# Attention pipeline of a macaron block: where the reciprocal, the cosine product and the side work stand

## The chip, the cores and the metric

The kernel runs on one core of a Trainium2 chip. The metric is the device time of one execution in microseconds (us), the median of several runs. All arithmetic is in 32-bit floating point.

Engines by their names in the profile: PE is TensorE (matrix products and transposes; PEld its weight loads), DVE is VectorE, ACT is ScalarE, POOL is GpSimd, SP is SyncE, which only issues transfers here. Each engine works through its own queue of instructions in the order in which the program wrote them.

## The reference

The input is x, 4 sequences of 512 tokens with 256 features. Three sublayers follow one another, each on a layer-normalised x:

```
x = x + 0.5 * ffn(layernorm(x))
x = x + attn(layernorm(x))
x = x + 0.5 * ffn(layernorm(x))
```

The feed-forward part is a mixture of 8 experts of width 512; each token goes to its best two:

```
logits = x @ gate;  w, idx = top_k(logits, 2);  w = softmax(w)
out = sum over e of combine[e] * (silu(x @ w0[e]) * (x @ w1[e])) @ wo[e]
```

The attention has 16 heads with low-rank queries, keys and values and a rotary part:

```
q   = rms_norm(h @ wq_a, q_w) @ wq_b          # per head 64 plain + 64 rotary
ckv = h @ wkv_a                               # 64 low-rank + 64 rotary keys, shared by the heads
kv  = rms_norm(ckv[..., :64], kv_w) @ wkv_b
attn = softmax(query . key * 128**-0.5);  out = (attn @ value) @ wo
```

## The kernel before

**Three stages.** A first feed-forward stage (up to some 300 us of the span), the attention (300 to 905 us), a second feed-forward stage. While attention runs, the routing of the second feed-forward stage is already worked out for batches whose attention is complete (a batch is one sequence of 512 tokens), and the next batch's keys and low-rank queries are prepared. This side work is cut into small parts that are strewn between the steps of attention.

**The attention loop** (L1543 to L1591) walks 64 items, a batch and a head each (`items`), and in each of them 4 places `kc`. Two heads make a pair; the place in the pair is `at`, 0 to 7, and a pair is the unit of the pipeline. In each place the loop writes, in this order:

- a block of scores (`put_scores`): 128 queries against 512 keys on PE, the negative maximum on DVE (L1352), the exponential on ACT (L1354), which also sums its row into `sm`. The block belongs to a head one to one and a half ahead (k = (i+1)*4 + 3 + kc). Place 1 has none, and place 0 has two.
- in place 0 of a pair, the weighing of the values of the two heads before (`put_weigh`, L1380, 16 matrix instructions of PE), its copy (L1444), and the division of the second head of this pair.
- four transposes of a head's probabilities on PE (L1367) and their copy from the accumulator memory, on DVE in even places (L1372), on ACT in odd places (L1374). There are two buffers for the transposes, so those of a place need the copy of two places earlier.
- a few parts of two lists of side work, `asked` and `beside`.

`put_divide(k)` does something only for the last of a head's four blocks, that is in places 0 and 4. It takes the reciprocal of `sm` on DVE (L1359), and four multiplications on POOL (L1361) make the exponentials into probabilities. The head that is divided in place 4 is the first of the next pair; its transposes begin in the next pair's place 0.

There are three buffers for the score blocks and the weighing together (`ps_a`), three for all side work in the accumulator memory (`ps_p`).

**Queries** (`asked`, six parts, added in place 1 for two pairs ahead): the products `pe` and `pn` on PE (L1319); then the cosine product on DVE (L1225) and a copy on ACT (L1326); then a lane shuffle on DVE (L1228) and the other copy; then, on POOL, the sine product (L1230) and two additions (L1232, L1234).

**In pairs with h % 4 == 1** (all even pairs but the very first) the output projection of four heads is written too, half in place 4 and half in place 6 (L1394, 8 matrix instructions each), and its addition on DVE (L1404) one place later.

**The list `beside`** (class `Beside`, L342 to L388) holds generators. `step(n)` runs up to n parts; each part says by what it yields when the next may run:

- a float is the price of the next part: it runs only in a place whose room (`ROOM[at]`) still has that much. Without a float the price is LITTLE, 0.2.
- an int n, or PE_NEXT, or PE_LATE: not before n places (one place for the two names) later.
- `PARTS[at]` is the largest number of parts of a place.

In the feed-forward stages the room is unlimited and `pe_places` names the places at which parts of PE may run; in the attention loop `pe_places` is empty.

From each batch's third head on `beside` is given, in this order: the routing of the batch before (`route_one`: layer norm with `normed`, gate, `choose`), the preparation of the next batch (`prepare`), the indirect writes of the routing (`scatter_one`: 8 small transfers of POOL, L515, each behind a small memset, only in places that are `quiet`), and in the last batch the list of tiles (`listing`, whose first instruction is the copy L888 and whose next is the PE instruction L894). Batch 0 has only the preparation of batch 1.

**Powers.** `inv_sqrt` (L403) takes a power -0.5 on POOL and yields 1; what reads it is the next part: `less` (L408) in `normed`, the product `low` (L1283) in `prepare`.

Of the kernel before, what the change touches and what calls it, by code (L numbers as in the profile page):

```python
# [42 lines left out]
def kernel(  # L43
# [21 lines left out]
    NT = S // P  # L65
# [270 lines left out]

    PE_NEXT, PE_LATE = "pe", "pe late"
    LITTLE = 0.2  # L340

    class Beside:  # L342
# [19 lines left out]
        def step(self, n=1):  # L362

            for _ in range(n):
                if not self.todo or self.count < self.until:
                    return
                if self.pe and self.pe_places:
                    n_ok = 1 if self.pe is PE_LATE else len(self.pe_places)
                    if self.place not in self.pe_places[:n_ok]:
                        return  # L370
                if self.cost > self.room:
                    return
                self.room -= self.cost
                said = next(self.todo[0], self)
                self.pe = said if said in (PE_NEXT, PE_LATE) else False
                self.cost = said if isinstance(said, float) else LITTLE
                if said is self:
                    self.todo.pop(0)
                elif self.pe or isinstance(said, int):
                    self.until = self.count + (1 if self.pe else said)  # L380

        def finish(self):
            self.quiet = True
# [55 lines left out]
    def normed(b, s, store=None, then=None, joint=False):  # L439


        mv = small.tile([P, NT, 2], F32, tag="mv", name="mv")
        if beside.room < math.inf:
            yield 1.2
        for t in range(NT):
            stats(mv, xs[b], t)
            if t % 2:
                yield 1.2 if t == 1 else LITTLE
        var = small.tile([P, NT], F32, tag="var", name="var")
        nc.vector.tensor_scalar_add(var, mv[:, :, 1], LN_EPS)  # L450
        rstd = small.tile([P, NT], F32, tag="rstd", name="rstd")
        yield from inv_sqrt(rstd, var, NT)
        less = minus_mean(mv, rstd)
        yield 0.8
        xn = [xp.tile([P, H2, D], F32, tag="xn", name="xn") for _ in range(2)]
        for half in range(2):
            norm_rows(xn[half], b, half, mv, rstd, less if half else None)
            if half == 0:

                yield 0.6  # L460
        if then is not None:
            then()
        if store is not None:
            for half in range(2):
                store_rows(nc.sync if store else nc.gpsimd, store, b, half, xn[half])
        s["xnT"] = tp.tile([P, DC, S], F32, tag="xnT", name="xnT")

        def turned(half):
            pt = ps_p.tile([P, DC, H2 * P], F32, tag="p", name="pt_ln")
            turn_rows(pt, xn[half])  # L470
            return pt

        def copied(half, pt):
            to = s["xnT"][:, :, half * H2 * P : (half + 1) * H2 * P]
            if half == 0:
                nc.scalar.copy(to, pt)
            else:
                nc.vector.tensor_copy(to, pt)

        yield PE_NEXT  # L480
        first = turned(0)
        if not joint:
            yield
            copied(0, first)
            yield
        second = turned(1)
        yield 0.7
        if joint:
            copied(0, first)
        copied(1, second)  # L490
        yield PE_NEXT
# [746 lines left out]
    def prepare(b):  # L1238

        s = st.setdefault(b, {})  # L1240
        if b == 0:
            nc.vector.tensor_scalar_mul(nwq, nwq, scale)
        yield from normed(b, s)

        pk = ps_p.tile([P, S], F32, tag="p", name="pk")
        for c in range(DC):
            nc.tensor.matmul(
                pk,
                lhsT=wkpe[:, c].rearrange("p u r -> p (u r)"),
                rhs=s["xnT"][:, c, :],  # L1250
                start=(c == 0),
                stop=(c == DC - 1),
            )
        s["k"] = [bp.tile([P, S], F32, tag=f"k{j}", name=f"k{j}") for j in range(2)]
        yield 0.7
        yield from rope(s["k"][1][:ROPE], s["k"][0][ROPE:], pk, xp, "xn")
        yield

        pj = ps_p.tile([P, NT, 2, RANK], F32, tag="p", name="pj")
        for t in range(NT):  # L1260
            for c in range(DC):
                nc.tensor.matmul(
                    pj[:, t].rearrange("p j r -> p (j r)"),
                    lhsT=s["xnT"][:, c, t * P : (t + 1) * P],
                    rhs=wqc[:, c, :],
                    start=(c == 0),
                    stop=(c == DC - 1),
                )
        yield
        sq = xp.tile([P, NT, 2, RANK], F32, tag="xn", name="sq")  # L1270
        nc.scalar.activation(sq, pj, AF.Square)
        yield 0.8
        rr = small.tile([P, NT * 2], F32, tag="rr", name="rr")
        nc.vector.tensor_reduce(
            rr, sq.rearrange("p t j r -> p (t j) r"), AX.X, ALU.add
        )
        ms = small.tile([P, NT * 2], F32, tag="ms", name="ms")
        nc.vector.tensor_scalar(ms, rr, 1.0 / RANK, RMS_EPS, ALU.mult, ALU.add)
        yield
        yield from inv_sqrt(rr, ms, NT * 2)  # L1280
        yield 0.7
        low = bp.tile([P, NT, 3, RANK], F32, tag="low", name="low")
        nc.vector.tensor_tensor(  # L1283
            low[:, :, :2, :],
            pj,
            rr.rearrange("p (t j) -> p t j", j=2).unsqueeze(3).to_broadcast([P, NT, 2, RANK]),
            ALU.mult,
        )
        yield
        nc.gpsimd.tensor_copy(low[:, :, 2, :], low[:, :, 0, :])  # L1290
        s["low"] = low

        s["q"] = bp.tile([P, S], F32, tag="lq", name="lq")
        for i in range(2):
            yield PE_NEXT
            pt = ps_p.tile([P, S], F32, tag="p", name="plow")
            for t in range(NT):
                nc.tensor.transpose(
                    pt[:, t * P : (t + 1) * P],
                    low[:, t, i : i + 2, :].rearrange("p j r -> p (j r)"),  # L1300
                    ident,
                )
            yield 0.7
            a, c = slice(0, RANK), slice(RANK, P)
            hq, hk = (a, c) if i == 0 else (c, a)
            nc.vector.tensor_scalar_mul(s["q"][hq], pt[hq], nwq[hq])
            yield 0.7
            nc.vector.tensor_scalar_mul(s["k"][1 - i][hk], pt[hk], nwk[hk])
        s["ready"] = True
# [103 lines left out]
    def put_queries(p):  # L1413

        if p < n_items // 2:
            b, h = items[2 * p]
            qs[p] = []
            yield from queries(b, h // 2, qs[p])
# [10 lines left out]
    def put_divide(k):  # L1429
        i, t = divmod(k, NT)  # L1430
        if i < n_items and t == NT - 1:
            divide(probs[i], sums.pop(i))
# [104 lines left out]


    PARTS = (5, 2, 1, 1, 1, 1, 1, 2)
    ROOM = (3.2, 1.2, 0.2, 0.2, 0.8, 1.2, 0.8, 1.2)  # L1540
    beside.pe_places = ()
    late = []
    for i, (b, h) in enumerate(items):  # L1543
# [13 lines left out]
        for kc in range(NT):  # L1557

            at = NT * (h % 2) + kc
            beside.at(at, at in (7, 0, 1, 2), LITTLE if late and ROOM[at] < 1.0 else ROOM[at])  # L1560
            k = (i + 1) * NT + LEAD + kc
            if at != 1 or i == 0:
                put_scores(k)
            if at == 0 and i > 0:

                put_scores(k + 1)
                put_weigh(i - 1, range(NT))
                put_divide(k)
                beside.step(PARTS[at])
            pts[i, kc] = turn_probs(probs[i], kc)  # L1570
            for f in late:
                f()
            late.clear()
            if at == 1:
                asked.add(put_queries(i // 2 + 2))
            elif at == 4 and h % 4 == 1 and i > 1:
                late.append(put_out(i - 2, 0))
            elif at == 6 and h % 4 == 1 and i > 1:
                late.append(put_out(i - 2, 1))
                late.append(lambda i=i: finish_x(i - 2))  # L1580
            if kc % 2 == 0:

                asked.step(2 if at == 4 else 1)
            if at != 0 or i == 0:
                put_divide(k)
            if kc % 2:
                asked.step()
            if at != 0:
                beside.step(PARTS[at])
        probs.pop(i)  # L1590
    beside.finish()  # L1591
# [86 lines left out]
```

## Time and profile before

| | us |
|---|---|
| median of 3 runs | 1150.05 (1148.97 to 1151.47) |
| the profiled execution | 1148.07 |
| its span, first to last instruction | 1146.3 |
| PE busy in the span | 1067.8 (93%) |
| POOL, DVE, ACT busy | 586.0, 557.9, 471.9 |
| mean granted clock of PE | 0.980 |

The starts of the query products L1319, one set per pair, give the length of each pair from its place 1 to the next pair's (us, the profiled execution):

| pair of the batch | 0 | 1 | 2 | 3 | 4 | 5 | 6 | 7 |
|---|---|---|---|---|---|---|---|---|
| batch 0 | 16.53 | 18.68 | 21.51 | 17.68 | 18.82 | 16.53 | 18.82 | 16.53 |
| batch 1 | 18.81 | 17.51 | 21.47 | 18.47 | 22.79 | 18.36 | 20.67 | 16.52 |
| batch 2 | 18.82 | 17.50 | 21.18 | 18.48 | 22.79 | 18.37 | 23.30 | 16.53 |
| batch 3 | 18.82 | 17.51 | 21.17 | 17.66 | 29.61 | | | |

A row of the profile's timeline reads: start and duration in us, engine, line and operation, result<-operands, shapes, and in brackets the idle time of the engine ahead of it with what ended that idle time. In a group of instructions the last figures are busy time, mean ns of one, idle time ahead and its releasers. A row of the table by stretches has, behind the stretch's length, the busy time of PE, PEld, DVE, ACT and POOL, the granted clock, the transfers' share and GB/s. PE's instructions overlap in their pipeline, so the duration of one is longer than the distance to the next.

### The profile page before, as it was taken

The page shows a single profiled execution, that of the slowest core. Times are in us where ns is not written, and L with a number is a line of the kernel's source. Part 1 is how long each engine was busy: PE and PEld are TensorE (multiplying, and loading weights), DVE is VectorE, ACT ScalarE, POOL GpSimd, SP SyncE. Part 2 cuts the span into 40 slices and gives each one's busy share as a digit, 9 for nine tenths or more (in the row PEclk, how much of TensorE's full clock was granted, in tenths as well). Part 3 has the DMA queues.
Part 4 walks back from the last instruction along what each step waited for, and adds up shares of the span by engine and source line. Part 5 has one row for each costly group of instructions (what it writes and reads, how often), then busy time and mean ns, then how long its engine had stood idle before and what let it go on. Part 6 is the DMA issues. An engine that isn't in the chain of part 4 may idle for free. (4 is left out here: it accounts for less than half of the span.)

```text
span 1146.3 us, 14713 instructions
## 1 busy us (share of the span) xinstructions
PE 1067.8 (93%) x4738; PEld 600.4 (52%) x4738; DVE 557.9 (49%) x1329; ACT 471.9 (41%) x1030; POOL 586.0 (51%) x655
## 2 busy tenths in 40 slices
PE   4898999999999999999999999999879999999995
PEld 3565555665445554455445545454444556655563
DVE  6453222234557465685656766456735343322221
ACT  4531431222555465645555555455535322144221
POOL 4344455456565455545664447754654236545542
PEclk8998999999999999999999999999989999999998
DMA  9963233322100000100000100001000224323432
GB/s 316 388 139 35 42 49 58 58 38 38 33 1 1 1 1 1 56 1 1 1 2 19 38 1 1 1 1 37 2 5 1 69 51 46 52 37 55 118 51 26
DMA packets 44043, 53.57 MB, mean 47 GB/s; under 512 B 10720, under 2 KB 36704, under 8 KB 43872
## 3 DMA queue, kind: packets, MB, share of 16 engines
q0 software_dynamic: 16960, 22.07, 12.4%
q1 hardware_dynamic: 26736, 30.55, 8.3%
q8 instruction: 40, 0.66, 0.2%
q14 instruction: 35, 0.29, 0.1%
q10 hardware_dynamic: 272, 0.01, 0.0%
HBM read 34.74 MB, written 22.07 MB: 50 GB/s over the span
## 5 line engine op out<-in xcount | busy, mean ns | idle before, releaser
L1344 PE MATMUL ps<-k,q 128*128 128x512 f32 x512 | 262.6, 605 | 5.8 <-POOL q L1232 5.0
L1093 PE MATMUL h<-w_sb,xT 128*128 (+1 forms) x576 | 263.5, 600 | 3.6 <-DVE xT L1061 3.1
L1352 DVE TENSOR_REDUCE nm<-ps 128x1 f32<-128x512 f32 x256 | 173.8, 685 | 92.7 <-PE ps L1344 88.6
L1354 ACT ACTIVATE pr<-ps,nm 128x512 f32<-128x512 f32 x210 | 144.2, 688 | 175.4 <-DVE nm L1352 158.6
L1361 POOL TENSOR_SCALAR pr<-pr,sm 128x512 f32<-128x512 f32 x210 | 142.4, 693 | 71.2 <-DVE sm L1359 51.9
L1367 PEld LDWEIGHTS pt<-ident,pr 128*128 128x128 f32 x840 | 102.1, 142 | 118.7 <-issue 65.3
L1093 PEld LDWEIGHTS h<-w_sb,xT 128*128 128x128 f32 (+1 forms) x576 | 101.4, 186 | 112.8 <-issue 103.4
L1142 POOL DMA_INDIRECT acc_d<-yo,idx x53 | 83.9, 1584 | 148.2 <-DVE yo L1165 74.7
L1129 DVE TENSOR_TENSOR it<-g,h 128x512 f32<-128x512 f32 x72 | 49.5, 688 | 223.7 <-PE h L1093 183.2
L1367 PE MATMUL pt<-ident,pr 128*128 128x128 f32 x840 | 137.7, 277 | 10.8 <-ACT pT L1374 10.2
L1137 ACT COPY iT<-pt_i 128x512 f32<-128x512 f32 x72 | 42.1, 585 | 241.5 <-PE pt_i L1135 241.5
L1093 PE MATMUL py<-w_sb,iT 128*128 (+1 forms) x576 | 136.9, 381 | 2.6 <-ACT iT L1137 1.4
L1230 POOL TENSOR_TENSOR tsin<-tsin,sin_sb 128x512 f32<-128x512 f32 x36 | 46.7, 1296 | 147.9 <-DVE tsin L1228 137.6
L1380 PE MATMUL po<-pT,low 128*64 128x512 f32 x512 | 118.0, 603 | 0.0
L1372 DVE COPY pT<-pt 128x512 f32<-128x512 f32 x128 | 87.3, 682 | 63.0 <-PE pt L1367 62.9
L1093 PEld LDWEIGHTS py<-w_sb,iT 128*128 128x128 f32 (+1 forms) x576 | 100.5, 184 | 19.6 <-ACT iT L1137 2.4
L1344 PEld LDWEIGHTS ps<-k,q 128*128 128x128 f32 x512 | 82.9, 192 | 43.6 <-ACT pT L1374 15.9
L1046 POOL DMA_INDIRECT xg<-xn_d,idx x72 | 72.2, 1003 | 32.4 <-issue 14.1
L1374 ACT COPY pT<-pt 128x512 f32<-128x512 f32 x128 | 74.3, 580 | 18.2 <-PE pt L1367 18.2
L1380 PEld LDWEIGHTS po<-pT,low 128*64 128x64 f32 x512 | 34.2, 138 | 79.9 <-issue 60.1
L1126 ACT ACTIVATE g<-h 128x512 f32<-128x512 f32 x72 | 43.0, 597 | 71.0 <-PE h L1093 67.9
L1165 DVE TENSOR_SCALAR yo<-py,wt 128x256 f32<-128x256 f32 x72 | 34.8, 483 | 65.5 <-PE py L1093 57.3
(234 smaller groups left out, 1328.3 us busy)
## 6 DMA issues: line engine op xcount, KB each, us to landing
w_sb<-in_L_ffn_w_kernel_dram SPq DMA_DIRECT2D x8, 1024.0 KB, 14.2
w_sb<-in_L_ffn_wo_kernel_dram SPq DMA_DIRECT2D x5, 1024.0 KB, 14.2
xn_d<-xn SPq DMA_DIRECT2D x12, 256.0 KB, 4.4
x<-_attn_hidden_states_dram SPq DMA_DIRECT2D x4, 512.0 KB, 9.4
x<-acc_d SPq DMA_DIRECT2D x4, 512.0 KB, 4.0
acc_d<-x SPq DMA_DIRECT2D x4, 512.0 KB, 3.0
out_dram<-acc_d SPq DMA_DIRECT2D x4, 512.0 KB, 6.1
xg<-xn_d,idx POOLq DMA_INDIRECT x72, 2.8
```

What stands on the lines that cost most here:

```text
L1046: nc.gpsimd.indirect_dma_start(out=xg[j], out_offset=None, in_=xn_d[f][: res["rows"], :], in_offset=bass.IndirectOffsetOnAxis(ap=res["idx" ...
L1093: nc.tensor.matmul(to[r], lhsT=lhsT[:, r], rhs=rhs, start=(k == 0), stop=(k == last - 1))
L1129: nc.vector.tensor_mul(it, g, ph[1])
L1142: nc.gpsimd.indirect_dma_start(out=dst, out_offset=bass.IndirectOffsetOnAxis(ap=idx, axis=0), in_=y, in_offset=None, compute_op=ALU.add,)
L1344: nc.tensor.matmul(ps, lhsT=qT[:, t * P : (t + 1) * P], rhs=st[b]["k"][h % 2], start=True, stop=True,)
L1352: nc.vector.tensor_reduce(nm, ps, AX.X, ALU.max, negate=True)
L1354: nc.scalar.activation(pr, ps, AF.Exp, bias=nm, accum_out=sm[:, t : t + 1])
L1361: nc.gpsimd.tensor_scalar(pr, pr, sm[:, t : t + 1], 1.0, ALU.mult, ALU.mult)
L1367: nc.tensor.transpose(pt[:, t * P : (t + 1) * P], probs[t][:, kc * P : (kc + 1) * P], ident)
L1372: nc.vector.tensor_copy(s, pt)
L1374: nc.scalar.copy(s, pt)
L1380: nc.tensor.matmul(po[j * RANK : (j + 1) * RANK], lhsT=st[b]["low"][:, kc, 1, :], rhs=pts[j], start=(kc == 0), stop=(kc == NT - 1),)
```

## The change

Six edits, all in the side work and in the order inside a place.

1. In place 5 `put_divide(k - 1)` is called right behind `put_scores`; the call in place 4 is gone. So the first head's reciprocal stands behind the next block's maximum on DVE.
2. The steps of `asked` are given by a table. The parts with the products and with the cosine product now both run in place 1, none in place 2, and all of them ahead of what `beside` does in that place, except in place 1, where `beside` goes first.
3. `ROOM` has other values, and the quiet places are 6, 7, 0, 1 instead of 7, 0, 1, 2.
4. PE_LATE waits two places where `pe_places` is empty, as in attention (in `choose` ahead of L634 and in `list_tiles` ahead of the last products).
5. `normed` yields ahead of each of the four statistics at 0.6 each, instead of two by two at 1.2, where the room is limited.
6. A part may yield a pair, (places, price). `prepare` does so ahead of `low`: one more place behind the power.

```diff
-                self.cost = said if isinstance(said, float) else LITTLE
+                self.cost = LITTLE
+                if isinstance(said, tuple):
+                    said, self.cost = said
+                elif isinstance(said, float):
+                    self.cost, said = said, None
                 if said is self:
                     self.todo.pop(0)
-                elif self.pe or isinstance(said, int):
-                    self.until = self.count + (1 if self.pe else said)
+                elif self.pe:
+                    late = said is PE_LATE and not self.pe_places
+                    self.until = self.count + (2 if late else 1)
+                elif said is not None:
+                    self.until = self.count + said
...
-        if beside.room < math.inf:
-            yield 1.2
+        small_parts = beside.room < math.inf
+        if small_parts:
+            yield 0.6
         for t in range(NT):
             stats(mv, xs[b], t)
-            if t % 2:
-                yield 1.2 if t == 1 else LITTLE
+            if small_parts or t % 2:
+                yield 0.6 if t < NT - 1 else LITTLE
...
         yield from inv_sqrt(rr, ms, NT * 2)
-        yield 0.7
+        yield 1, 0.7
...
-    ROOM = (3.2, 1.2, 0.2, 0.2, 0.8, 1.2, 0.8, 1.2)
+    ROOM = (3.2, 0.8, 0.7, 0.2, 0.8, 1.4, 0.8, 1.4)
+    ASKED = (0, 2, 0, 1, 2, 1, 0, 0)
...
-            beside.at(at, at in (7, 0, 1, 2), LITTLE if late and ROOM[at] < 1.0 else ROOM[at])
+            beside.at(at, at in (6, 7, 0, 1), LITTLE if late and ROOM[at] < 1.0 else ROOM[at])
...
                 put_divide(k)
                 beside.step(PARTS[at])
+            if at == 5:
+                put_divide(k - 1)
             pts[i, kc] = turn_probs(probs[i], kc)
...
             if at == 1:
                 asked.add(put_queries(i // 2 + 2))
+                beside.step(PARTS[at])
...
-            if kc % 2 == 0:
-                asked.step(2 if at == 4 else 1)
-            if at != 0 or i == 0:
+            asked.step(ASKED[at])
+            if at == 0 and i == 0:
                 put_divide(k)
-            if kc % 2:
-                asked.step()
-            if at != 0:
+            if at > 1 or at == 0 and i == 0:
                 beside.step(PARTS[at])
```

## The prediction

> **What bounds the kernel now.** First the page's table of engines: TensorE is busy for 93% of the span, no other engine over 51%. The edits all lie in the attention stage, so next the groups by line for 300 to 895 us, sorted by the idle time ahead of TensorE's instructions:
>
> ```profile
> PE 1067.8 (93%) x4738; PEld 600.4 (52%) x4738; DVE 557.9 (49%) x1329; ACT 471.9 (41%) x1030; POOL 586.0 (51%) x655
> L1344 PE MATMUL ps<-k,q 128*128 128x512 f32 x504 | 258.7, 605 | 5.0 <-POOL q L1232 5.0
> L1367 PE MATMUL pt<-ident,pr 128*128 128x128 f32 x816 | 133.9, 277 | 10.4 <-ACT pT L1374 10.2
> L634 PE MATMUL pr<-cut,ones 128*128 128x32 f32 x6 | 1.2, 286 | 4.6 <-DVE cut L623 4.6
> L894 PE MATMUL pn_c<-ones,cut 128*128 128x1 f32 x2 | 0.6, 362 | 6.4 <-DVE cut L888 6.4
> ```
>
> TensorE sets the pace, and about 30 us of this stage are its idle time, in four kinds. What is to be won or lost is there, and in the clock that falls behind an idle stretch.
>
> I took the start of each pair's query products (L1319) as a mark. Without other work a pair lasts 18.82 us when output projections run in it and 16.53 when not ("even" and "odd" pairs from here). The timeline of an odd pair (389 to 426 us), VectorE, ScalarE and TensorE:
>
> ```profile
> 400.36 0.69 DVE L1352 TENSOR_REDUCE nm<-ps 128x1 f32<-128x512 f32 x1 [1.86 <-PE ps L1344]
> 401.57 0.68 DVE L1225 TENSOR_TENSOR tcos<-pe,cos_sb 128x512 f32<-128x512 f32 x1
> 402.17 0.68 DVE L1352 TENSOR_REDUCE nm<-ps 128x1 f32<-128x512 f32 x1
> 404.00 0.68 DVE L1372 COPY pT<-pt 128x512 f32<-128x512 f32 x1
> 405.58 0.18 DVE L1359 RECIPROCAL sm<-sm 128x4 f32<-128x4 f32 x1 [0.91 <-ACT pr L1354]
> 405.68 1.27 DVE L1352 TENSOR_REDUCE nm<-ps 128x1 f32<-128x512 f32 x2
> 406.45 0.69 ACT L1354 ACTIVATE pr<-ps,nm 128x512 f32<-128x512 f32 x1 [0.90 <-DVE nm L1352]
> 407.13 0.58 ACT L1374 COPY pT<-pt 128x512 f32<-128x512 f32 x1
> 407.76 0.66 PE L1367 MATMUL pt<-ident,pr 128*128 128x128 f32 x4 [0.75 <-ACT pT L1374]
> ```
>
> The reciprocal of place 4 stands on VectorE 0.91 us until the exponential has summed; the maximum of place 5, whose scores were ready at 404.2, waits behind it, then its exponential, then ScalarE's copy of place 5, then place 7's transposes.
>
> **The change part by part.** A usual step of TensorE is 1.30 us (scores at 400.60, 401.90, 403.19). In the odd pair only two steps are longer: place 5 to 7 took 2.27 (0.97 over), place 3's took 1.50 (0.20 over; place 5's transposes wait for place 3's copy on ScalarE). All else in 16.53 is work of TensorE.
>
> *Reciprocal behind the next maximum.* The maximum starts when VectorE's copy ends, 404.65 instead of 405.68. The exponential of place 5 then follows that of place 4 (404.78 to 405.55) at once, not at 406.45; the copy is over near 406.9 instead of 407.7, and TensorE would reach place 7's transposes at 406.84. That is 0.88 of the 0.97. The reciprocal itself waits for the same sum, so it ends no later than about 405.6; its four GpSimd multiplications (2.69) are wanted by transposes 4.5 us after their end. If that cover were gone, each us of delay would cost one.
>
> *Cosine product one place earlier.* On VectorE the product (0.60 of issue time), on ScalarE the copy L1326 (0.57), move behind the query products (end 399.27). VectorE idles 1.86 us before the maximum at 400.36 and ScalarE 2.26, so both fit; nothing is added to the path. Behind the waiting product stands that maximum; if the products came over 0.4 us late the maximum would be late by the rest. It frees 0.6 us of VectorE in places 2 and 3, which recovers the 0.20 and gives the step above its margin. Even pairs gain nothing: their two projections (1.73 each) already hide this chain.
>
> So 1.17 us for each odd pair. Six odd pairs have no other work (three in batch 0, one each later; the last pair has no scores left): 6 x 1.17 = 7.0. Ten have routing or preparation work beside them; there VectorE work now falls on place 4 (normalised rows 1.08, one set of row statistics 0.6, the `low` product 0.69), just ahead of the maximum that was freed. Bounds 0 and 1.17 each; I take 0.9, since TensorE's own side work there (0.44 per four transposes) hides part: 9.0.
>
> *Indirect writes at places 6, 7, 0, 1.* Going through the yields with the new room, the eight writes of batches 1 and 2 fall 2, 2, 1, 2, 1 on places 0, 1, 6, 7, 0, where before they fell 4, 2, 1 on 0, 1, 2 and one on 7. What the crowd costs, from the timelines of GpSimd and TensorE:
>
> ```profile
> 729.59 0.97 POOL L515 DMA_INDIRECT tab_d<-cut  x1 [0.19 <-issue]
> 730.58 1.29 POOL L1230 TENSOR_TENSOR tsin<-tsin,sin_sb 128x512 f32<-128x512 f32 x1
> 736.44 1.26 POOL L1232 TENSOR_TENSOR q<-tcos,tsin 64x512 f32<-64x512 f32 x1 [4.57 <-DMA tab_d<-cut]
> 737.75 1.69 PE L1344 MATMUL ps<-k,q 128*128 128x512 f32 x2 [2.57 <-POOL q L1232]
> ```
>
> The first addition of the query turn waits until the last write issued has landed. Seven writes at 1.27 each end about 9 us after the multiplications; four end 3.8 us earlier and land before TensorE wants the queries. This removes 1.59 + 2.57 + 0.87 (three batches), and the clock loss after the second: its scores took 1.69 and its weighing 4.74, against 1.12 and 3.65, 1.66 in all. Sum 6.7; I take 6.0.
>
> [...]
>
> In the last batch the list of tiles follows the writes directly:
>
> ```profile
> 840.50 1.03 POOL L515 DMA_INDIRECT tab_d<-cut  x1 [0.16 <-issue]
> 843.99 0.23 DVE L888 COPY cut<-run 128x128 f32<-128x128 f32 x1 [10.96 <-DMA tab_d<-cut]
> 844.27 0.58 PE L894 MATMUL pn_c<-ones,cut 128*128 128x1 f32 x2 [6.39 <-DVE cut L888]
> 844.71 2.05 PE L1344 MATMUL ps<-k,q 128*128 128x512 f32 x2
> 840.00:860.00 20.00, 15.73 (x58) 10.51 (x59) 10.72 (x21) 6.13 (x15) 7.83 (x10) 0.74 0.03 7
> ```
>
> The list's first copy (L888) waits for the last write to land, with everything of VectorE behind it. By my count two writes fall in place 1 of pair 3, three in places 6 and 7, three in place 0 of pair 4, and the copy still in that place 0. Before, one write stood there. So the last write is issued two writes (2.5 us) later, and L894 now comes ahead of the query products (1.06), which no longer fill the wait. Earlier queries take some of GpSimd's backlog away. Landing after the issue's start was 2.8 to 9.0 us over all writes, 3.5 here. Bounds -1 and +9; I take +4. The clock of 0.74 in that stretch (0.26 x 20 / 0.5, some 10.4 us at half speed) follows the idle time before and after the change alike, so it enters with nothing.
>
> *Two places for late TensorE work; statistics in four parts; the power's reader a place later.* L634's wait (3 x 1.54 = 4.6) comes from VectorE's small additions one place ahead:
>
> ```profile
> 652.04 1.98 DVE L623 TENSOR_TENSOR cut<-cut 128x8 f32<-128x8 f32 x3
> 654.08 0.41 PE L634 MATMUL pr<-cut,ones 128*128 128x32 f32 x2 [1.54 <-DVE cut L623]
> ```
>
> It goes. But that part (2.4 us of VectorE) now stands at place 6 ahead of place 7's maximum, and the three parts behind L634 (0.9, 0.4, 1.9) all fall in the next place 0, after the weighing, ahead of VectorE's copy that place 2's transposes need. I put about 1.3 and 0.8 on TensorE per batch, together 0.5 more than the 1.54: +1.5 in three batches (bounds -4.6, nothing given back, and +12, all 5.6 us of it exposed). The power's later reader ends VectorE's wait at L1283 (2.3 us before in three batches), mostly hidden: -1.0. The preparation ends by pair 6, two pairs ahead of its reader, so its lateness costs nothing. The feed-forward stages keep their order: room is unlimited there, places are given, and `low` falls on the same place after the power.
>
> **The sum.** -7.0 - 9.0 - 6.0 + 4.0 + 1.5 - 1.0 = -17.5 us. The profiled span is 1146.3 (1148.07 with what lies around it) and becomes 1128.8; the runs' median, 1150.05, is 2.0 above the profiled run, and becomes **1132.5**.
>
> **Rivals.** *Work beside takes the gain back.* The ten loaded odd pairs gain nothing (+9.0 on the sum) and the routing costs 1.5 more per batch (+4.5): 1146, or 1140 if only half of it. For it: VectorE has about 1.5 us free between places 2 and 7 of an odd pair (7.8 of TensorE against 6.3), and `low` with two query scalings is 2.1. Against: TensorE has work of its own there.
>
> *All fits.* Routing costs nothing and returns 4.6 (-6), ten pairs gain in full (-2.7), the list waits no longer (-4): 1120. For it: the small operations take 0.2 when GpSimd is quiet (L623's fourth at 654.05, 0.17). Against: the count of writes.
>
> *Slower: the routing in one place becomes the bound.* If TensorE sees all of the 5.6 us in each of the three later batches, 16.8, and the list's copy its upper 9, this is 16.8 - 1.5 + 5 more than the sum: 1153. It would decide from about 6 us per batch. For it: nothing on VectorE can pass these parts. Against: it idles 3.2 us in each place 0, where most of them fall.
>
> *It doesn't do what it says.* Were the maximum held by something else, the 16 odd pairs would keep their time (+16): 1148.5, no change. Against: the rows above name the exponential's sum, and scores done 1.4 us sooner.
>
> **Chances.** Forecast 0.55, work takes it back 0.22, all fits 0.10, slower 0.08, no effect 0.05. The forecast's own range is 1127 to 1138. The range 1123 to 1145 leaves out the slow and the idle case and the ends of two others. Runs of this kernel tell no change from 0.2% (2.3 us): faster by more 0.88, within 0.05, slower 0.07.
>
> **What would show it.** Odd pairs near 15.4 us instead of 16.53, L1374 gone as releaser of L1367, the reciprocal behind the maximum with the idle before it still there; L1232 without waits of 3 us and more; L634's wait gone but waits before L1380 near it; L888's wait at least as long as before. The prediction is wrong if odd pairs stay over 16.2 us, or if one wait of the routing exceeds 6 us in every batch.

## The result, and the profile after

The changed kernel takes 1131.9 us (median of 4 runs, 1130.57 to 1136.96) against 1149.69 for the kernel before: a ratio of 0.985, 95% interval 0.982 to 0.988. In a second measurement on another chip it was 1135.34 against 1153.08, 0.984 (0.981 to 0.986). The profiled span is 1129.1 instead of 1146.3 us, 17.2 less; 17.5 had been forecast.

The engines over the whole span of the changed kernel, and the groups of TensorE in its attention stage (300 to 877 us). The lines shown here stand 9 higher than before: L1353 is the scores (L1344 before), L1376 the transposes (L1367), L1389 the weighing (L1380), L643 the routing's product (L634), L903 the list's product (L894).

```profile
PE 1059.7 (94%) x4738; PEld 601.4 (53%) x4738; DVE 562.7 (50%) x1329; ACT 476.4 (42%) x1030; POOL 586.5 (52%) x655
L1353 PE MATMUL ps<-k,q 128*128 128x512 f32 x501 | 255.6, 602 | 0.0
L1376 PE MATMUL pt<-ident,pr 128*128 128x128 f32 x816 | 132.1, 275 | 3.8 <-ACT pT L1383 3.8
L1389 PE MATMUL po<-pT,low 128*64 128x512 f32 x480 | 109.6, 598 | 4.8 <-ACT pr L1363 4.6
L643 PE MATMUL pr<-cut,ones 128*128 128x32 f32 x6 | 1.2, 276 | 0.0
L903 PE MATMUL pn_c<-ones,cut 128*128 128x1 f32 x2 | 0.6, 362 | 11.2 <-DVE cut L897 11.2
```

Of the four kinds of idle time two have shrunk (transposes 10.4 to 3.8, scores 5.0 to 0), one has moved (the routing's 4.6 is now 4.8 ahead of the weighing) and one has grown (the list, 6.4 to 11.2).

An odd pair without other work, VectorE, ScalarE and TensorE in the timeline:

```profile
396.07 0.69 DVE L1234 TENSOR_TENSOR tcos<-pe,cos_sb 128x512 f32<-128x512 f32 x1 [0.87 <-PE pn L1328]
397.06 0.69 DVE L1361 TENSOR_REDUCE nm<-ps 128x1 f32<-128x512 f32 x1 [0.30 <-PE ps L1353]
400.33 0.68 DVE L1381 COPY pT<-pt 128x512 f32<-128x512 f32 x1
400.95 0.69 DVE L1361 TENSOR_REDUCE nm<-ps 128x1 f32<-128x512 f32 x1
401.79 0.18 DVE L1368 RECIPROCAL sm<-sm 128x4 f32<-128x4 f32 x1
402.42 0.57 ACT L1383 COPY pT<-pt 128x512 f32<-128x512 f32 x1
403.35 0.60 PE L1376 MATMUL pt<-ident,pr 128*128 128x128 f32 x4
```

The cosine product stands in VectorE's idle time ahead of the maximum at 397.06. The maximum of place 5 (400.95) follows the copy at once, the reciprocal stands behind it; ScalarE's copy of place 5 ends at 402.99, and place 7's transposes start at 403.35 without a wait. From one step to the next TensorE takes 1.30 us, from 397.30 to 403.79.

The lengths of the pairs, measured as before the change:

| pair of the batch | 0 | 1 | 2 | 3 | 4 | 5 | 6 | 7 |
|---|---|---|---|---|---|---|---|---|
| batch 0 | 15.37 | 19.30 | 21.07 | 16.44 | 18.82 | 15.37 | 18.82 | 15.36 |
| batch 1 | 18.82 | 18.15 | 21.25 | 17.18 | 22.80 | 16.99 | 18.81 | 15.37 |
| batch 2 | 18.82 | 18.15 | 20.95 | 17.17 | 22.81 | 16.98 | 18.83 | 15.36 |
| batch 3 | 18.82 | 18.16 | 20.97 | 27.15 | 21.70 | | | |

Added up, "the stretch" from here on: from pair 0 of batch 0 to pair 5 of batch 3 it is 561.44 us before and 545.79 after, 15.65 less. It is the measure for the experiments. Outside it the profiles differ by chance: it began at 304.92 in the kernel before, at 303.84 in the changed one, and between 303.0 and 305.4 in the first four experiments, whose code up to there orders the same work.

### The profile page after: what moved, and what is told of

It is laid out like the page before. It is cut to its first block, busy times and chain, and to the rows that moved or that the text cites. A ratio compares the mean times of both kernels' runs of the same rounds, so it can differ in the third digit from the quotient of the medians.

```text
span 1129.1 us, 14709 instructions
## 1 busy us (share of the span) xinstructions
PE 1059.7 (94%) x4738; PEld 601.4 (53%) x4738; DVE 562.7 (50%) x1329; ACT 476.4 (42%) x1030; POOL 586.5 (52%) x655
## 5 line engine op out<-in xcount | busy, mean ns | idle before, releaser
L1353 PE MATMUL ps<-k,q 128*128 128x512 f32 x512 | 260.7, 602 | 0.8 <-ACT pr L1363 0.8
L1376 PEld LDWEIGHTS pt<-ident,pr 128*128 128x128 f32 x840 | 103.3, 142 | 104.3 <-issue 65.1
L1376 PE MATMUL pt<-ident,pr 128*128 128x128 f32 x840 | 135.9, 275 | 4.1 <-ACT pT L1383 3.8
L1389 PE MATMUL po<-pT,low 128*64 128x512 f32 x512 | 116.9, 598 | 4.8 <-ACT pr L1363 4.6
L1353 PEld LDWEIGHTS ps<-k,q 128*128 128x128 f32 x512 | 82.6, 191 | 44.8 <-issue 21.0
L1389 PEld LDWEIGHTS po<-pT,low 128*64 128x64 f32 x512 | 33.9, 136 | 83.5 <-issue 56.5
```

The costliest lines, as they stand in the source:

```text
L1353: nc.tensor.matmul(ps, lhsT=qT[:, t * P : (t + 1) * P], rhs=st[b]["k"][h % 2], start=True, stop=True,)
L1376: nc.tensor.transpose(pt[:, t * P : (t + 1) * P], probs[t][:, kc * P : (kc + 1) * P], ident)
L1389: nc.tensor.matmul(po[j * RANK : (j + 1) * RANK], lhsT=st[b]["low"][:, kc, 1, :], rhs=pts[j], start=(kc == 0), stop=(kc == NT - 1),)
```

## The experiments

Spans are of one profiled execution each; beside r1 to r4, on their chip, the span of the kernel before was 1149.7.

**r1_recip, edit 1 alone**, in the kernel before:

```diff
+            if at == 5:
+                put_divide(k - 1)
             pts[i, kc] = turn_probs(probs[i], kc)
...
-            if at != 0 or i == 0:
+            if at == 0 and i == 0:
                 put_divide(k)
```

> The kernel before with edit 1 alone: the first head's reciprocal behind the maximum of place 5. Theory (the wait for the exponential's sum holds that maximum): an odd pair without other work falls from 16.53 us to about 15.65, the 0.97 us at place 7 all but gone and the 0.20 at place 5 still there; span some 10 us shorter, 1136. Rival (VectorE is simply full there, so the wait only passes to the maximum of place 6): odd pairs stay near 16.5, span within 2 us of 1146.

Free odd pairs 15.56, span 1137.7, stretch 551.33 (-10.1). The theory holds, the rival falls: the wait for the sum did hold the maximum.

**r2_asked, edit 2 alone**, in the kernel before; the reciprocal stays in place 4:

```diff
+    ASKED = (0, 2, 0, 1, 2, 1, 0, 0)
...
                 asked.add(put_queries(i // 2 + 2))
+                beside.step(PARTS[at])
...
-            if kc % 2 == 0:
-                asked.step(2 if at == 4 else 1)
-            if at != 0 or i == 0:
+            asked.step(ASKED[at])
+            if at == 4 or at == 0 and i == 0:
                 put_divide(k)
```

> The kernel before with edit 2 alone: cosine product and first copy in place 1, the reciprocal still in place 4. Theory: the exponential of place 4 comes 0.6 us earlier and with it the sum, the reciprocal and the maximum behind it; together with the 0.20 an odd pair falls to about 15.75, so that edits 1 and 2 overlap and don't add. Rival (only the 0.20 is recovered, the reciprocal holds the rest): 16.33.

Free odd pairs 16.03, between the two values; span 1135.8, stretch 551.81 (-9.6). VectorE's timeline in such a pair, and the wait at place 7 that is left in the next such pair, shows why:

```profile
400.14 0.68 DVE L1372 COPY pT<-pt 128x512 f32<-128x512 f32 x1
401.59 0.18 DVE L1359 RECIPROCAL sm<-sm 128x4 f32<-128x4 f32 x1 [0.77 <-ACT pr L1354]
401.68 1.27 DVE L1352 TENSOR_REDUCE nm<-ps 128x1 f32<-128x512 f32 x2
...
438.62 0.66 PE L1367 MATMUL pt<-ident,pr 128*128 128x128 f32 x4 [0.44 <-ACT pT L1374]
```

The reciprocal still waits (0.77 instead of 0.91) and still holds the maximum, but all of it lies earlier against TensorE. The edits overlap: an odd pair gains 0.97 and 0.50 by each alone and 1.16 by both.

**r3_both, edits 1 and 2**, all side work as before.

> The kernel before with edits 1 and 2, all side work as before. Theory: odd pairs at 15.36 as in the changed kernel, the four waits on the indirect writes still there (1.6, 2.6, 0.9 and 6.4 us of TensorE) and L634's three waits of 1.5; span 1146.3 less some 7 for the six free pairs and some 9 for the ten loaded, 1130. Rival (the order inside the place gains only with the new places of the side work): span above 1138.

Free odd pairs 15.37, span 1128.4, stretch 544.69 (-16.75): more than the whole change gains. The waits on the writes are still there, and one expectation was wrong: L634's wait has shrunk to 0.28 to 0.40 without edit 4.

```profile
490.91 0.41 PE L634 MATMUL pr<-cut,ones 128*128 128x32 f32 x2 [0.28 <-DVE cut L623]
572.24 1.12 PE L1344 MATMUL ps<-k,q 128*128 128x512 f32 x2 [1.40 <-POOL q L1232]
825.99 0.59 PE L894 MATMUL pn_c<-ones,cut 128*128 128x1 f32 x2 [5.78 <-DVE cut L888]
```

The routing's additions stand behind maxima on VectorE; with the cosine product out of places 2 and 3 they come earlier (r1 alone left 1.44 of the wait, r2 alone 0.58 to 0.89).

**r4_side, edits 3 to 6**: the changed kernel with the order inside a place as before (`put_divide` in place 4, the old steps of `asked`, `beside` last).

> The kernel before with edits 3 to 6 (room, quiet places, two places for late work, statistics, power), the order inside a place as before. Theory: odd pairs stay at 16.53; the writes give back about 6 us, the list's wait costs about 4 to 5 more, the routing changes one wait for another: span 1144 to 1148. Rival (the side work makes half of the gain): span near 1138.

Span 1148.0, stretch 561.48 (0.0 against before). Odd pairs keep 16.53; pairs 6 of batches 1 and 2 fall to 18.82, so the 6.3 us of the writes are won; the list's wait is 9.19 instead of 6.39. Loaded pairs lost the rest: pair 1 takes 18.5 instead of 17.5, pair 2 22.2 to 23.4 instead of 21.2 to 21.5. The rival falls: the side work's edits gain nothing on balance.

**r5_late1, the changed kernel with PE_LATE at one place**:

```diff
-                    self.until = self.count + (2 if late else 1)
+                    self.until = self.count + 1
```

> The changed kernel with PE_LATE back at one place. Theory (the 2.4 us of small VectorE operations of the routing, standing in place 6, are the cost, and the second place only moves it): TensorE waits 1.5 to 2 us at L643 (the line of L634 in this kernel) in each of three batches instead of 1.5 at L1389, span within 2 us of 1129.1. Rival (the second place is a gain of its own): 1.5 more per batch, span 1133 to 1135.

r5 to r8 ran on another chip, where the kernel before takes 1163.5; there 592 to 595 us lie outside the stretch, against 583 in the first profile of the changed kernel. The free pairs have the same length, 15.37, so the stretch counts: 553.06, 7.3 more than 545.79. Pair 2, where the routing stands, has its old length (21.31, 21.02, 21.01 against 21.25, 20.95, 20.97): waits of 1.0 to 1.3 and 0.2 at L643 instead of 1.5 to 1.6 at L1389. There the theory holds, but it missed the loss in pair 3. With every later part a place or more ahead, the power falls behind GpSimd's multiplications and its last addition, and `less`, which reads it, stops VectorE ahead of a maximum. VectorE, then TensorE in batches 1 and 2:

```profile
520.12 0.16 DVE L416 SCALAR_TENSOR_TENSOR less<-mv,rstd 128x4 f32<-128x4 f32 x1 [3.80 <-POOL rstd L411]
...
521.75 3.65 PE L1389 MATMUL po<-pT,low 128*64 128x512 f32 x16 [3.37 <-ACT pr L1363]
673.45 5.35 PE L1389 MATMUL po<-pT,low 128*64 128x512 f32 x16 [3.34 <-ACT pr L1363]
```

So the second place doesn't remove the routing's cost; its worth here is that it keeps the parts behind it at places where they don't wait.

**r6_gap, six places between the last write and what follows**:

```diff
                 ph.scatter(s, k, t)
-                yield
+                yield 6 if k and t == NT - 1 and not beside.pe_places else None
```

> The changed kernel with six places between the last indirect write of a batch and what follows in the list. Theory (the list's copy waits for nothing but the landing of that write): the wait of 11.2 us at L903 goes, the half clock behind it too (13.65 us before, some 4 to 5 us of TensorE's time after its return): span 1129.1 - 11.2 - 4.5, near 1113. Rival (the tiles' list is late for another reason, or the pair's own multiplications are late anyway): at most 5 us gained, 1124 or more.

Stretch 531.38, 14.4 below the changed kernel; 15.7 had been expected (the span, 1126.0, is of the slower chip and can't be set against 1113). Pairs 3 and 4 of batch 3 take 15.37 and 19.16 instead of 27.15 and 21.70. The list's copy and product no longer wait:

```profile
834.75 0.43 DVE L897 COPY cut<-run 128x128 f32<-128x128 f32 x1
839.18 0.38 PE L903 MATMUL pn_c<-ones,cut 128*128 128x1 f32 x2
```

**r7_last7, the routing's additions in place 7**, on top of r6: ahead of them the part yields 1.0, which the room of place 6 (0.8) refuses and that of place 7 (1.4) takes, and `PE_LATE` behind them becomes PE_NEXT in the attention loop.

```diff
-            yield 0.8
+            yield 0.8 if k == 0 else 1.0
...
-        yield PE_LATE
+        yield PE_LATE if beside.pe_places else PE_NEXT
```

> As the one before, with the routing's part of small additions in place 7, behind that place's maximum, instead of place 6, and L643 one place later, so where it was. Theory: the waits of 1.5 at L1389 go in three batches, since only the maxima of place 0 stand behind that part: 4.6 us less than the one before, span near 1108. Rival (VectorE is short over the whole pair): the wait reappears at the next pair's transposes, 0 to 1 us gained.

Stretch 527.44, 3.9 less than r6 (4.6 expected). In batches 1 to 3 pair 2 falls from between 20.94 and 21.23 to between 19.37 and 19.66, no wait of 1.5 is left at L1389, and pair 3 takes 0.1 to 0.3 more. Ratio to the kernel before 0.966 (0.964 to 0.968), median 1123.86.

**r8_pairs, edits 1 and 2 with two writes in a place**: r3, the quiet places 6, 7, 0, 1, a wait of one place after every second write and of six after the last.

> Edits 1 and 2 with the room of before, and of the rest only the quiet places 6, 7, 0, 1; at most two indirect writes in a place, and six places behind the last. Theory: the waits 1.40, 2.15, 2.44 at the scores and 5.78 at L894 go, with them most of the half clock of batch 3 (10.2 us): span 1128.4 - 11.8 - 3 = near 1113.5. Rival (the queries' additions wait for the landing however few the writes): 1 to 2 us per batch remain, 1117.

Stretch 529.06, 15.6 less than r3 (14.9 expected of the span); ratio 0.967 (0.965 to 0.968), median 1123.87. One wait on the addition is left, 1.64 in pair 3 of batch 3.

**r9_far, writes in places 6 and 7 only**: edits 1 and 2, no other wait between the writes, and six places ahead of the list.

> As r8, but writes only in places 6 and 7 (three of each pair over three pairs), and the six places only ahead of the list. Theory (the addition in place 4 waits for the landing of the writes issued ahead of it, and only their nearness makes that a wait of TensorE): the addition keeps its semaphores but no longer waits, and the 1.64 of TensorE at the scores in pair 3 of batch 3 goes; from pair 0's query products of batch 0 to pair 5's of batch 3, 529.1 us in r8, it is 527.5. Rival (the addition is late because GpSimd is full in that pair): 529 or more, with the wait still there.

Stretch 526.73, the lowest. The 1.64 is gone; GpSimd in the pair behind the first three writes:

```profile
815.64 0.96 POOL L515 DMA_INDIRECT tab_d<-cut  x1 [0.19 <-issue]
821.42 1.27 POOL L1233 TENSOR_TENSOR tsin<-tsin,sin_sb 128x512 f32<-128x512 f32 x1 [2.09 <-DVE tsin L1231]
822.77 1.27 POOL L1235 TENSOR_TENSOR q<-tcos,tsin 64x512 f32<-64x512 f32 x1
```

The addition comes 6.2 us after the last write's end and doesn't wait. Median 1120.12, ratio 0.9705 (0.9677 to 0.9733).

**r10_after, the changed kernel beside r9.**

> The changed kernel itself beside r9 on one chip. Theory: its ratio to the kernel before is again near 0.985, and its pairs have the lengths of the first profile; r9 is 16 to 20 us below it. Rival (the gain of the change depends on the chip): a ratio off by more than 0.005.

1135.34, ratio 0.984 (0.981 to 0.986); stretch 545.34 (545.79 in the first profile), with 6.0 us more outside it. r9 is 15.2 us faster on that chip, a little under the 16 to 20 expected. r7 and r9, 527.4 and 526.7 in the stretch, weren't timed on one chip; which is faster stays open. r7, r8 and r9 all have a shorter stretch than the changed kernel, by 16.7 to 19.1 us.

## Why the prediction was right

The forecast of 1132.5 met 1131.9, and the direction and the main cause were right. That it met it so closely is partly luck. In the stretch the forecast was 16.3 (17.5 less the sixth free pair, which lies behind it) against 15.65, with errors of -2.5 and +1.8 that largely cancel; and 1.08 of the span's 17.2 lies ahead of the stretch, where the profiles differ by chance. Where the 15.65 us of the stretch came from, by the pairs' lengths before and after:

| | forecast | measured |
|---|---|---|
| free odd pairs (five of the six lie in the stretch) | 5.85 | 5.81 |
| loaded pairs 1, 2, 3, 5, with routing and power | 7.6 | 5.1 |
| pairs 6 of batches 1 and 2 (writes) | 5.1 | 6.3 |
| pairs 3 and 4 of batch 3 (writes, list) | -2.2 | -1.6 |

(The forecast's terms are split over the rows: a loaded pair 0.9, and the wait of 0.87 and one loaded pair in batch 3's row.)

- **Reciprocal and cosine product.** 1.17 a pair was forecast, 1.16 measured; r1, r2 and r3 show both parts at work, and that the chain of waits was read rightly.
- **Ten loaded odd pairs, 9.0.** This term was mis-sized: the nine that can be read without the list's wait gained 4.0 where 8.1 had been taken. Pairs 3 and 5 gained 1.2 to 1.4 (0.44 of it, in pairs 3 of batches 1 and 2, is four transposes that moved to pair 4), but pairs 1 lost 0.62 to 0.65, below the lower bound of nothing gained. TensorE has the same instructions in pair 1 as before, so the loss is all waiting. The rival "work beside takes the gain back" was right for this pair: edits 3 and 5 put the normalised rows into place 4, ahead of the freed maximum, and there they took 1.69 us; in the kernel before the same two rows took 0.73. The timeline of batch 1, VectorE, GpSimd and TensorE:

```profile
469.31 1.69 DVE L429 TENSOR_SCALAR xn<-x,mv,rstd 128x256 f32<-128x256 f32 x2
469.57 1.27 POOL L1241 TENSOR_TENSOR q<-tcos,tsin 64x512 f32<-64x512 f32 x1
470.91 0.68 DVE L1361 TENSOR_REDUCE nm<-ps 128x1 f32<-128x512 f32 x1
...
472.99 0.33 PE L1376 MATMUL pt<-ident,w_sb 128*128 128x128 f32 x1 [0.54 <-ACT pT L1383]
```

  The second of the two rows began 0.05 us after GpSimd's first addition and ended 0.15 us after it: 1.37 us instead of 0.41. It is so in all four batches (1.37 to 1.38 us each); the other eight rows of the attention stage took 0.40 to 0.41. This is read from the overlap; no run moved the addition alone. r3, with these parts at their old places, has 17.11 in pair 1.
- **Writes.** The spreading was forecast right, write by write, and so was its effect: no wait of TensorE on the queries is left. GpSimd in batch 1:

```profile
563.33 0.96 POOL L524 DMA_INDIRECT tab_d<-cut  x1 [0.19 <-issue]
567.91 1.27 POOL L1241 TENSOR_TENSOR q<-tcos,tsin 64x512 f32<-64x512 f32 x1 [2.10 <-DMA tab_d<-cut]
```

  The addition still waits, 2.1 instead of 3.6, but it ends long before its scores. The size was 6.3 in the two pairs against 5.1, but 1.66 of it is the half clock of the kernel before (0.50 for 3.41 us from 738.18); r1 and r3, with gaps of 2.37 and 2.15 us at that place, had none (last section).
- **List.** The wait grew from 6.39 to 11.20, +4.8 where +4 was taken, by the mechanism named: two more writes behind the multiplications, and the query products now behind the list's product. GpSimd, VectorE and TensorE, and the stretch of 20 us:

```profile
822.90 0.96 POOL L524 DMA_INDIRECT tab_d<-cut  x1 [0.19 <-issue]
827.13 0.23 DVE L897 COPY cut<-run 128x128 f32<-128x128 f32 x1 [14.51 <-DMA tab_d<-cut]
827.41 0.59 PE L903 MATMUL pn_c<-ones,cut 128*128 128x1 f32 x2 [11.20 <-DVE cut L897]
820.00:840.00 20.00, 12.59 (x48) 7.59 (x49) 8.91 (x18) 5.02 (x12) 6.73 (x11) 0.69 0.03 8
```

  In r6, with six places for the landing, the wait is gone. The clock's zero held roughly: half clock lasted 10.24 us before and 13.65 after, but TensorE worked through only 6.6 and 5.0 us of it.
- **Routing.** The wait did change its place as forecast (1.5 to 1.6 ahead of the weighing, 1.3 forecast; the 0.8 behind it didn't come), and r7 shows that place 6 was the cause. The forecast's reason for the old wait was incomplete: r2 and r3, where it shrinks without edit 4, show that the cosine product in front made most of it. So edit 2 would have removed most of this wait without edit 4.
- **Power.** VectorE's wait at L1283 stood in two batches, 1 and 2, 1.17 us each, not in three, and it is gone. Pair 5, where it stood, takes 16.98 against 17.31 in r3, so edits 3 to 6 together won at most 0.7 there, where 1.0 was taken. Against it `less` now waits 2.98 and 2.96 us for its power in pair 3 of the same batches, with no wait of TensorE behind it.
- **Signs.** Two of those named did not come. ScalarE's copy still releases the transposes for 3.8 us, all in loaded pairs, and the reciprocal has next to no idle time ahead of it (401.64 to 401.79): without the cosine product in front the sum is there earlier. In r1, which leaves that product where it was, it waits 0.31.
- **What the sum hid.** r3 and r4 show that edits 1 and 2 alone gain 16.75 us of the stretch and edits 3 to 6 alone nothing; in the whole change these cost 1.1. My terms for the side work added up to a gain of 1.5; in fact they cost 1.1.

## What to carry to other kernels

Where an engine works through its queue in order, an instruction that waits for a late sum belongs behind the next instruction whose inputs are ready, if its own reader has slack: moving one reciprocal by one place gave 0.97 us a pair. Side work is best measured by what stands behind it in the queue, not by how much of it fits in a pair: 1.6 us of small operations (VectorE from 494.42 to 496.01 in the changed kernel) cost 1.3 us a batch more ahead of a maximum that the weighing waits for than one place later (r6 against r7). And before a part that overwrites the source of a transfer, as the list's first copy does here (its tile shares the one buffer `cut`), leave the transfer the time to land: six places were worth 14 us.

## What the runs showed of the hardware

**The length of a gap alone did not tell whether the clock fell.** In r5 two weighings stand behind gaps of 3.37 and 3.34 us (rows above): the first runs at full rate (3.65), the second takes 5.35. The stretches of 20 us around them (the granted clock is the third figure from the end):

```profile
515.00:535.00 20.00, 16.43 (x76) 8.55 (x75) 10.01 (x20) 10.82 (x26) 10.23 (x13) 1.00 0.00 1
665.00:685.00 20.00, 16.46 (x70) 7.72 (x69) 9.29 (x22) 9.69 (x24) 9.29 (x12) 0.91 0.00 0
```

In r2 a gap of 1.97 us, ahead of the scores of pair 6 in batch 2, brought the clock down (the weighing behind it took 5.28); in r1 one of 2.37 at the same place didn't (3.65). The stretches of 20 us around those two gaps, r2 and then r1:

```profile
720.00:740.00 20.00, 18.03 (x75) 8.87 (x74) 9.58 (x17) 8.25 (x20) 11.31 (x15) 0.91 0.01 1
```

```profile
720.00:740.00 20.00, 17.63 (x79) 9.60 (x78) 8.94 (x16) 8.95 (x21) 13.80 (x20) 1.00 0.01 2
```

In the attention stage half clock (0.50) lasted 3.41 us from 738.18 and 10.24 from 840.58 in the kernel before, and 13.65 from 818.79 in the changed one. What else decided it was not shown; no run was made for it. The 1.66 us that the prediction booked for the clock were therefore no sure gain: at the same place the gap of 2.57 in the kernel before and that of 1.97 in r2 brought the clock down, those of 2.37 in r1 and 2.15 in r3 (weighing 3.65, clock 1.00 from 715 to 735) didn't.

**The addition's wait for the writes is in the program, not in the chip.** GpSimd's first addition reads no table and yet waited for the writes to land, 3.6 us in batch 1 of the kernel before. The built program of the kernel before names their semaphores at that instruction, beside GpSimd's own:

```
L1230 TensorTensor tsin<-tsin,sin_sb 128x512 [waits DVE_49]
L1232 TensorTensor q0_4733<-tcos,tsin 64x512 [waits DMASW3_49,DMASW4_49,DMASW2_49,DMASW5_49,DMASW1_49,DMASW6_49,DMASW0_49,Pool_49]
```

It is the instruction that waits for GpSimd's own progress, and the transfers that GpSimd issued ahead of it are waited for with it; that one brings the other is argued from this list and wasn't tried. r9 shows that distance makes it harmless: there the addition comes 6.2 us after the last write's end and doesn't wait.
